# A new issue plan for a fused macaron block: the sums of squares placed behind GpSimd's additions, the copies of V's windows one step earlier

## The chip, the cores and the metric

One core of one Trainium2 chip. The metric is the device time of one execution in microseconds (us), the median of several runs. The engines are PE (TensorE; its weight loads are listed as PEld), DVE (VectorE), ACT (ScalarE), POOL (GpSimd) and SP (SyncE, which issues nearly all DMAs here). Each engine runs its own instructions strictly in the order in which the program lists them, and waits at an instruction until the semaphores that it names are reached.

## The reference: what is computed

`x` is 2048 tokens by 128 features. Three blocks are added to it in turn: half of a 6-layer local-attention transformer, a linear-attention block with a GELU feed-forward, and half of the same 6-layer transformer again (the same weights). So there are 12 attention layers, 6 before the linear block and 6 behind it.

```python
x = x + 0.5 * ffn_ref(layernorm(x), ...)    # 6 layers
x = x + attn_ref(layernorm(x), ...)         # linear attention, ELU+1 features
x = x + 0.5 * ffn_ref(layernorm(x), ...)    # 6 layers
# one layer of ffn_ref: 16 heads of 64, window 32
q, k, v = split(shift_tokens(x) @ Wqkv)
q, k = l2norm(q) * qs, l2norm(k) * ks ; rotary tables on both
out = local_attention(q, k, v)    # a window sees itself and the one before
x = out @ Wo + x
x = (a * gelu(gate)) @ W2 + b2 + x          # a, gate = LN(shift(x)) @ W1 + b1
```

Everything is fp32.

## The kernel before, in words

**Tiling.** Features lie on the partitions, tokens along the free dimension. A layer is worked off in 8 chunks of 256 tokens (`c`), a chunk in 4 steps; a step is one half of the heads (`h8`) of one tile of 128 tokens (`t`). So a layer has 32 steps. Feed-forward and norms go by chunks of 512 tokens (`f`).

**What one chunk does**, with the plan's names in brackets:

- `project` [proj], lines 274-324: Q and K by 8 matmuls per call, the rotary products on DVE (L298), their additions on POOL (L304), the squares on ACT (L310), the addition of the two halves of the squares on POOL (L324).
- `square_sums` [ss], L326-336: 4 matmuls add the squares over each head. `norms`, L398-412: the inverse root on ACT and DVE. `spread_norms` [rk], L428-442: two small DMAs to DRAM (L434), four back that spread them (L439).
- `gather` [gq0, gq1], L390: two DMAs of 256 KB each put the rotated queries into head order (`hq`). `scale_keys` [sk0, sk1]: one DVE multiplication (L448), then four DMAs of 128 KB (`hk`, L396).
- `values_proj` [vproj]: V by matmul (L348), copied by ACT (L352). `values_windows` [vwin], L354-375: eight DMAs (L368-L371) that copy V into the layout of the windows (`vw`, two buffers).
- `similarities` [sim], `exponentials` [e0, e1], `normalised` [nrm], `transposed` [te], `values` [av] and `output` [out]: scores on PE (L476, L486), maxima on DVE (L498), exponentials on ACT (L511), their scaling on POOL (L523), transposes on PE (L536), the product with V on PE (L563, which reads `vw`), the projection by `wo` (L579), and the residual on DVE (L588). In a layer's last call `output` also loads the next layer's `wo` (L136).
- `feed_forward` [ff, ff2, ff3] in 17 pieces; its norm has the mean (L211), the square on ACT (L215) and the variance matmul (L218).

**What sets the order.** No scheduler moves anything: the order is written out by hand in the table `POS`. A piece with the entry `(s, p)` goes to step `t0 + s`, and within a step the pieces are issued in the order of `p`:

```python
def at(step, pos, fn, *args):
    plan.setdefault(step, []).append((pos, len(plan.get(step, ())), fn, args))
...
put("ss", t0 + 2 * g2, square_sums, l, c, g2)
put("vwin", t0 + 2 * t, values_windows, l, c, t)
...
for step in sorted(plan):
    for _, _, fn, args in sorted(plan[step], key=lambda it: it[:2]):
        fn(*args)
```

`p` only ranks pieces; a changed `p` matters where it moves a piece past another one that uses the same engine (or issues a DMA on SP, or takes a PSUM buffer from the same pool of five, `ps_small`). SP's list holds 34 DMAs per chunk, and each DMA also waits for the one eight places ahead of it to land, because eight semaphores are used in turn. Between layers 5 and 6 lie the linear block's pieces `sums0`-`sums3`, `kv`, `outs0`-`outs3`; this stretch is called the hand-over below.

Of the kernel before, what the change touches and what calls it, by code (L numbers as in the profile page):

```python
# [30 lines left out]
HID = 512  # L31
LN_EPS = 1e-5
POS = {
    "tabq": [(-11, 115), (-10, 177)],
    "tabk": [(-9, 9), (-9, 156)],
    "ss": [(-7, 141)],
    "vwin": [(1, 68)],
    "gq0": [(-6, 126)],
    "gq1": [(-4, 58)],
    "e0": [(0, 84)],  # L40
    "e1": [(0, 85)],
    "nrm": [(1, 67)],
    "qn": [(-3, 111)],
    "ek": [(-1, 82)],
    "proj": [(-9, 137), (-8, 31), (-8, 32), (-8, 33), (-8, 37), (-8, 140)],
    "vproj": [(-2, 21), (-2, 80)],
    "norms": [(-4, 35), (-4, 73), (-4, 110)],
    "rk": [(-4, 193), (-3, 20)],
    "sk0": [(-2, 81)],
    "sk1": [(-1, 83)],  # L50
    "te": [(2, 53), (2, 55)],
    "av": [(2, 132), (2, 179), (2, 180)],
    "out": [(4, 71), (4, 119)],
    "sim": [(0, 65), (0, 66), (0, 67)],
    "ff": [(11, 88), (12, 26), (12, 92), (13, 5), (13, 159), (14, 93), (15, 128), (15, 148),
        (16, 13), (17, 108), (17, 125), (18, 23), (18, 47), (18, 48), (18, 151), (21, 131),
        (21, 187)],
    "ff2": [(12, 113), (13, 16), (13, 168), (14, 57), (14, 163), (15, 103), (15, 133), (16, 39),
        (16, 105), (16, 108), (16, 109), (16, 185), (16, 189), (17, 28), (17, 63), (17, 86),
        (17, 89)],  # L60
    "ff3": [(10, 171), (10, 172), (10, 174), (10, 182), (10, 186), (10, 190), (11, 2), (11, 14),
        (11, 19), (11, 27), (11, 112), (11, 114), (11, 117), (11, 124), (11, 142), (11, 170),
        (11, 170)],
    "start0": [(-19, 75), (-16, 60), (-16, 77), (-16, 90), (-13, 30), (-11, 130)],
    "start1": [(-10, 134), (-9, 145), (-7, 87), (-7, 146), (-7, 154), (-6, 12)],
    "start2": [(-8, 56), (-7, 62), (-5, 36), (-5, 192), (-4, 96), (-4, 165)],
    "start3": [(-4, 34), (-4, 38), (-4, 79), (-4, 107), (-3, 4), (-3, 22)],
    "sums0": [(-9, 18), (-9, 104), (-8, 122), (-8, 155), (-8, 161), (-7, 61), (-7, 123),
        (-6, 24)],
    "sums1": [(-1, 106), (-1, 178), (0, 64), (0, 69), (1, 6), (1, 66), (2, 150), (2, 172)],  # L70
    "sums2": [(1, 173), (1, 188), (2, 157), (2, 191), (3, 54), (3, 129), (3, 149), (4, 100)],
    "sums3": [(3, 183), (4, 11), (4, 43), (4, 70), (4, 72), (4, 120), (4, 120), (4, 181)],
    "kv": [(5, 3)],
    "outs0": [(5, 8), (5, 10), (5, 74), (5, 97), (5, 139), (5, 166), (6, 59), (6, 176), (7, 158),
        (7, 162), (8, 51), (8, 52), (8, 121), (8, 135)],
    "outs1": [(6, 50), (11, 46), (11, 99), (12, 15), (13, 1), (13, 44), (13, 169), (14, 42),
        (14, 152), (15, 25), (15, 41), (15, 98), (15, 138), (16, 40)],
    "outs2": [(6, 144), (13, 74), (13, 95), (13, 153), (14, 101), (14, 136), (14, 167), (15, 45),
        (15, 127), (15, 184), (16, 76), (16, 78), (16, 116), (17, 29)],
    "outs3": [(5, 118), (15, 164), (16, 17), (16, 102), (17, 49), (17, 91), (18, 7), (18, 94),  # L80
        (18, 151), (19, 47), (19, 143), (19, 147), (19, 160), (19, 175)],
}
EXP_LN = "natural_log_exp_and_others"

# [867 lines left out]
```

## Time and profile before

| | |
|---|---|
| median of 3 runs | 3533.92 us (3528.49 to 3537.05) |
| the profiled execution's own time | 3530.32 us |
| its span, first to last instruction | 3528.3 us |
| granted TensorE clock, mean | 0.979 |
| DVE, ACT, POOL busy | 74%, 78%, 63% of the span |
| one step, from one layer's `wo` load to the next (629.20 to 898.12 us, 32 steps) | 8.40 us |
| mean time of one DMA issue on SP | about 0.6 us (L368 to L371: medians 554 to 595 ns) |

The waits view names for each engine what it waited for, with the sum, the count and the longest. The timeline lists instructions in order of time: start, duration, engine, line, operation, output<-input, and in brackets the idle time before it and what ended that. On SP the duration is that of issuing a DMA, not of its landing.

### The profile page before, as it was taken

What the parts mean: (1) busy time and instruction counts of PE and PEld (TensorE: products, weight loads), DVE (VectorE), ACT (ScalarE), POOL (GpSimd) and SP (SyncE); (2) the same over time, 40 slices, a digit from 0 to 9 for tenths busy, and PEclk for the clock granted to TensorE, in tenths of its full rate; (3) what the DMA queues carried; (4) which work ended last, traced back from release to release, by engine and by line L of the source; (5) the groups of instructions that cost most, each with busy time, mean ns of one, the idle gap of its engine ahead of it and who ended that gap; (6) DMA issues with size and microseconds to landing.
All of it is one profiled execution on the core that took longest, in us unless ns stands there. A gap on an engine that the chain in (4) does not pass through costs nothing. (4 is left out here: it accounts for less than half of the span.)

```text
span 3528.3 us, 153591 instructions
## 1 busy us (share of the span) xinstructions
PE 3300.5 (94%) x64088; PEld 2299.6 (65%) x64088; DVE 2623.4 (74%) x4924; ACT 2738.8 (78%) x8805; POOL 2228.7 (63%) x2195
## 2 busy tenths in 40 slices
PE   6999999999999999998677999999999999999997
PEld 3766666666666676676335766766666766766664
DVE  5777877777777787786337777877778777777784
ACT  3787877888887887887546788888888788888886
POOL 5676666667666667663136666666667676666661
PEclk8999999999999999999789999999999999999999
DMA  4555565556556556555003556555565565565552
GB/s 121 132 147 139 128 149 144 130 144 150 130 145 148 132 143 151 137 130 129 24 12 94 138 138 147 134 142 143 134 154 133 135 156 135 134 154 131 137 137 72
DMA packets 356445, 459.91 MB, mean 130 GB/s; under 512 B 52396, under 2 KB 218664, under 8 KB 355752
## 3 DMA queue, kind: packets, MB, share of 16 engines
q1 hardware_dynamic: 355752, 450.11, 52.4%
q8 instruction: 504, 8.26, 1.0%
q14 instruction: 189, 1.55, 0.1%
HBM read 96.53 MB, written 2.62 MB: 28 GB/s over the span
## 5 line engine op out<-in xcount | busy, mean ns | idle before, releaser
L511 ACT ACTIVATE e<-sim,st,rq 128x64 f32<-128x64 f32 x3072 | 1194.8, 411 | 307.4 <-DVE st L499 294.5
L298 DVE TENSOR_TENSOR prod<-p,tab 128x1024 f32<-128x1024 f32 x768 | 933.3, 1220 | 196.9 <-ACT sq L310 100.8
L304 POOL TENSOR_TENSOR abq<-prod 128x512 f32<-128x512 f32 x384 | 491.4, 1280 | 743.9 <-DVE prod L298 625.0
L289 PE MATMUL p<-xa,wqk 128*128 128x256 f32 x3072 | 783.7, 399 | 12.0 <-DVE xa L243 6.4
L324 POOL TENSOR_TENSOR sq<-sq 128x256 f32<-128x256 f32 x768 | 669.9, 892 | 1.0
L511 ACT ACTIVATION_READ_ACCUMULATOR e<-sim,st,rq 128x1 f32 x3072 | 649.4, 211 | 0.0
L289 PEld LDWEIGHTS p<-xa,wqk 128*128 128x128 f32 x3072 | 563.7, 193 | 104.0 <-issue 11.2
L310 ACT ACTIVATE sq<-p 128x512 f32<-128x512 f32 x768 | 438.3, 611 | 217.0 <-PE ss L332 109.6
L304 POOL TENSOR_TENSOR abk<-prod 128x512 f32<-128x512 f32 x384 | 496.1, 1292 | 117.2 <-DVE prod L298 113.4
L563 PEld LDWEIGHTS av<-eT,vw 64*64 64x64 f32 x18432 | 397.3, 135 | 196.1 <-DVE xf L588 34.1
L523 POOL TENSOR_TENSOR e<-e,st 128x512 f32<-128x512 f32 x384 | 400.2, 1042 | 137.7 <-DVE st L521 113.1
L348 PE MATMUL pv<-wv,xa 128*128 128x512 f32 x768 | 415.0, 622 | 60.7 <-ACT gate L619 57.1
L563 PE MATMUL av<-eT,vw 64*64 64x32 f32 x18432 | 442.6, 221 | 30.7 <-DMA vw<-v 13.0
L579 PE MATMUL y<-oT,wo 128*128 128x128 f32 x3072 | 394.1, 282 | 0.2 <-DVE oT L572 0.2
L563 PE MATMUL av<-eT,v 64*64 64x32 f32 x6144 | 392.6, 220 | 1.0 <-issue 0.9
L579 PEld LDWEIGHTS y<-oT,wo 128*128 128x128 f32 x3072 | 357.7, 192 | 18.6 <-issue 1.0
L448 DVE TENSOR_TENSOR abk<-abk,rk 128x1024 f32<-128x1024 f32 x192 | 349.3, 1819 | 2.9 <-issue 0.7
L498 DVE TENSOR_REDUCE sim<-sim 128x4 f32<-128x256 f32 x768 | 309.4, 403 | 29.0 <-PE sim L486 28.7
L486 PE MATMUL sim<-hk,hq 64*32 64x64 f32 x24576 | 330.9, 223 | 0.0
L536 PEld LDWEIGHTS te<-sq_consts,e 128*128 128x128 f32 x1536 | 188.6, 141 | 210.9 <-issue 156.1
L563 PEld LDWEIGHTS av<-eT,v 64*64 64x64 f32 x6144 | 325.9, 135 | 0.0
L572 DVE COPY oT<-av 128x256 f32<-128x256 f32 x384 | 161.3, 420 | 211.9 <-PE av L563 207.1
(139 smaller groups left out, 4574.3 us busy)
## 6 DMA issues: line engine op xcount, KB each, us to landing
hq<-abq SPq DMA_DIRECT2D x384, 256.0 KB
hk<-abk SPq DMA_DIRECT2D x768, 128.0 KB
vw<-v SPq DMA_DIRECT2D x768, 128.0 KB
rk<-rkd SPq DMA_DIRECT2D x384, 128.0 KB
vw<-v SPq DMA_DIRECT2D x744, 64.0 KB
wqk<-in_Wqk SPq DMA_DIRECT2D x48, 256.0 KB
tab<-in_rot SPq DMA_DIRECT2D x24, 512.0 KB
wv<-in_Wv SPq DMA_DIRECT2D x24, 256.0 KB
```

Of the source, the lines that this page charges most:

```text
L289: nc.tensor.matmul(both[s][:, u, :], wqk[g][:, 2 * s + u, :], xs, start=True, stop=True)
L298: nc.vector.tensor_tensor(prod, both[s].unsqueeze(2).to_broadcast([P, 2, 2, AC]), tabs[l, s].rearrange("p (u v) t -> p u v t", u=2), ALU.mult,
L304: nc.gpsimd.tensor_tensor(d["qk"[s], g // 2][:, :, g % 2, :], prod[:, 0], prod[:, 1], ALU.add)
L310: nc.scalar.activation(sq, both[s], AF.Square)
L324: nc.gpsimd.tensor_tensor(sq[:, 0, :], sq[:, 0, :], sq[:, 1, :], ALU.add)
L348: nc.tensor.matmul(ps, xa[:, ti * P : (ti + 1) * P], wv[j], start=True, stop=True)
L448: nc.vector.tensor_tensor(k, k, r.unsqueeze(1).to_broadcast([P, 2, CH]), ALU.mult)
L486: nc.tensor.matmul(sims[par][WIN * b : WIN * b + WIN, i, :], d["hq"][rows, 4 * h8 + i, at : at + WIN], d["hk"][rows, 4 * h8 + i, at : at + ...
L511: nc.scalar.activation(e[:, i, par, :], d["sims", step][par][:, i, :], AF.Exp, bias=st8[:, 0, i, par : par + 1], scale=rq[:, i, par : par ...
L523: nc.gpsimd.tensor_tensor(ef, ef, st8[:, 1].rearrange("p i r -> p (i r)").unsqueeze(2).to_broadcast([P, 8, SK]), ALU.mult,)
L563: nc.tensor.matmul(av[u][r : r + 64, m, WIN * b : WIN * b + WIN], d["vs", t][u][b][:, at : at + DH], d["eT", step][64 * u : 64 * u + 64, i ...
L579: nc.tensor.matmul(y[:, 0:P], wo[:, i, :], d["oT", t].rearrange("p h u m q -> p (h u m) q")[:, i, :], start=(i == 0), stop=(i == 7),)
```

## The change

Only the table `POS` changes. Many ranks are merely renumbered. What lies at another place in the step, or in another step, is below (the pieces that every chunk uses, and the pieces of the feed-forward, the start and the linear block whose order against others changes):

```diff
-    "ss": [(-7, 141)],
-    "vwin": [(1, 68)],
-    "gq0": [(-6, 126)],
+    "ss": [(-7, 188)],
+    "vwin": [(0, 68)],
+    "gq0": [(-6, 87)],
...
-    "sk1": [(-1, 83)],
+    "sk1": [(-1, 164)],
...
-    "out": [(4, 71), (4, 119)],
+    "out": [(4, 100), (4, 120)],
...
-    "ff": [(11, 88), (12, 26), (12, 92), (13, 5), (13, 159), (14, 93), (15, 128), (15, 148),
+    "ff": [(11, 88), (12, 30), (12, 92), (13, 5), (13, 156), (14, 94), (15, 128), (15, 144),
...
-    "start2": [(-8, 56), (-7, 62), (-5, 36), (-5, 192), (-4, 96), (-4, 165)],
+    "start2": [(-9, 163), (-7, 35), (-5, 41), (-5, 192), (-4, 9), (-4, 111)],
...
-    "outs1": [(6, 50), (11, 46), (11, 99), (12, 15), (13, 1), (13, 44), (13, 169), (14, 42),
-        (14, 152), (15, 25), (15, 41), (15, 98), (15, 138), (16, 40)],
-    "outs2": [(6, 144), (13, 74), (13, 95), (13, 153), (14, 101), (14, 136), (14, 167), (15, 45),
-        (15, 127), (15, 184), (16, 76), (16, 78), (16, 116), (17, 29)],
+    "outs1": [(6, 51), (11, 85), (11, 99), (12, 15), (13, 1), (13, 47), (13, 167), (14, 46),
+        (14, 148), (15, 29), (15, 45), (15, 98), (15, 137), (17, 44)],
+    "outs2": [(6, 105), (13, 74), (13, 95), (13, 149), (14, 96), (14, 161), (14, 165), (14, 183),
+        (15, 103), (15, 127), (16, 75), (16, 77), (16, 117), (17, 33)],
```

Set side by side, the two programs hold the same instructions. In the order of each engine: on PE 49 of 37,494 rows stand elsewhere, 44 of them variance matmuls of the feed-forward's norm (L218) that now precede the eight `y` matmuls (L579) instead of following them; on DVE 15 of 4,926, on ACT 6 of 5,735, on POOL 27 of 2,200 (24 of them are the zero fills of `vw`, L366; all other moves on these three engines lie at the start and around the hand-over); on SP at least 1,188 of 3,405. The 4 matmuls of `ss` stand at the same place of PE's order as before, except three times in the hand-over. SP's order for one chunk, by steps modulo 4 (8+4 means so many DMAs):

| step | before | after |
|---|---|---|
| 0 | gq1 2, rk to DRAM 2 | gq1 2, **vwin of tile 0: 8**, rk to DRAM 2 |
| 1 | rk back 4, vwin of tile 0: 8 | rk back 4 |
| 2 | sk0 4, gq0 2 (a layer's `wo` load ahead of them) | **vwin of tile 1: 8**, sk0 4, gq0 2 (the `wo` load behind them) |
| 3 | vwin of tile 1: 8, sk1 4 | sk1 4 |

## The prediction

> **What bounds the kernel now.** I read the page first, then PE's busy time by stretches, then what PE waited for, then the timeline of SP, because the edits move mostly DMAs.
>
> The page's first part and two stretches from the view by windows (columns: time, PE, PEld, DVE, ACT, POOL busy with counts, clock, DMA share, GB/s):
>
> ```profile
> PE 3300.5 (94%) x64088; PEld 2299.6 (65%) x64088; DVE 2623.4 (74%) x4924; ACT 2738.8 (78%) x8805; POOL 2228.7 (63%) x2195
> ```
> ```profile
> 400.00:700.00 300.00, 290.15 (x5847) 206.44 (x5845) 232.76 (x442) 248.16 (x802) 199.67 (x196) 1.00 0.57 139
> ...
> 1640.00:1940.00 300.00, 229.56 (x2344) 129.28 (x2342) 154.13 (x260) 165.13 (x393) 117.09 (x120) 0.85 0.21 52
> ```
>
> PE is busy 290 of 300 us in the layers, but only 230 of 300 around the hand-over. So an edit in the layers is worth at most the gaps that it closes on PE, about 3% of the stretch. The waits view of PE says who ended those gaps (sum, times, longest):
>
> ```profile
> PE pv L348 <- ACT gate L619: 57.1, 75, 1.4
> PE ss L332 <- POOL sq L324: 30.5, 21, 5.3
> ...
> PE av L563 <- DMA vw<-v: 13.0, 16, 1.6
> ```
>
> The reader sees three candidates. The first is a PSUM buffer that the GELU frees; no edit touches it. The second is the wait that the change's name speaks of; in the layers it is small (3.4 us between 100 and 1640, 2.7 us between 1940 and 3440; the rest lies at the start, 17.0, and in the hand-over). The third is the copy of V's windows, and it is an edit's target. The timeline of SP shows why `vw` comes late:
>
> ```profile
> 600.34 1.17 SPq L390 DMA_DIRECT2D hq<-abq  x2
> 601.56 0.71 SPq L368 DMA_DIRECT2D vw<-v  x1
> ...
> 607.24 0.59 SPq L371 DMA_DIRECT2D vw<-v  x1
> 607.93 2.53 SPq L396 DMA_DIRECT2D hk<-abk  x4
> 610.56 1.90 SPq L390 DMA_DIRECT2D hq<-abq  x2
> 612.56 1.92 SPq L434 DMA_DIRECT2D rkd<-rn  x2
> 615.85 2.09 SPq L439 DMA_DIRECT2D rk<-rkd  x4
> ```
>
> `vw` of tile 1 stands behind gq0 (600.34), whose buffer comes free only when the scores of step 3 are done. Its last DMA is issued from 607.24 to 607.83, and `av`, which reads it, starts at 611.02: 3.2 us for a landing. The chain of waits has two such landings, of 2.37 and 4.26 us, so the lead is used up:
>
> ```profile
> 1938.28 2.37 DMA vw<-v
> 1940.65 0.04 issue
> 1940.69 1.01 PE av L563 x54
> ```
>
> **The change, part by part.**
>
> *ss.* Its four matmuls follow the same PE instruction as before in every layer; what it was moved past (copies of `av` on ACT and DVE, L570 and L572) are other engines' work. Cost 0; below nothing and above it too, because PE's order and POOL's additions are the same.
>
> *vwin one step earlier.* No instruction is added; eight DMAs per tile leave their place. Tile 1 now stands behind rk's return (ends 617.94) and ahead of sk0, so it needs only the copy of V and the `av` of step 1 that frees its buffer; it is ready about 1.5 steps, 12 us, sooner. Tile 0 stands behind gq1 instead of behind rk's return, some 6 us sooner by the rows above. Queued behind it on SP are the `rkd` DMAs, which need DVE's `rn`. Eight issues of 0.6 us are 4.8 us; with vwin of tile 1 gone from in front of sk1, sk1 and gq1 can go once DVE's multiplication is done (603.5), so gq1 ends about 607.3 and vwin at 612.1, against 612.56 for `rkd` today. So nothing behind it is later. What goes: PE's 13.0 us on `vw`. Ends: 0 (the next of `av`'s inputs, `eT` or a PSUM buffer, is as late) and 13.0. PE's own previous instruction had ended before each of these gaps and DVE's `eT` appears with only 4.3 us over 5 gaps, so I take **-11**. ACT also waited 33.2 us for `vw` (its copy of V must not overwrite a buffer that is still being read) and POOL 112.1; both engines are idle over 20% of the span, so these count 0 in the sum and are kept for a rival.
>
> *sk1, gq0.* DVE's order is unchanged. sk1's four DMAs stand eight issues nearer the front, gq0 waits for the same scores as before. 0.
>
> *The variance matmul ahead of `y`, 44 times.* Its input, ACT's `lnsq`, ends 2.6 us before the `y` that it now precedes. `y` ends 1.0 us later (the matmul's length), and behind it DVE's residual add. The timeline of DVE shows the cover:
>
> ```profile
> 644.54 0.59 DVE L588 TENSOR_TENSOR xf<-y,xa 64x128 f32<-64x128 f32 x2
> 646.87 0.42 DVE L572 COPY oT<-av 128x256 f32<-128x256 f32 x1 [1.74 <-PE av L563]
> ```
>
> DVE idles 1.74 us right after it; 0.7 us of cover remains. Cost 0; without that cover it would be 44 times 1.0 us on DVE, not on PE. PSUM buffers change owners with this swap: some `av` now take the one that ACT's copy of V frees, whose end is over 1 us ahead of `av` in the median step of those classes. 0.
>
> *The zero fills of `vw` on POOL*: 24 of 0.516 us, earlier by five POOL instructions, in a step without `ss`. 0.
>
> *The next layer's `wo` load*, moved from ahead of sk0 to behind gq0. Today it is issued at 629.20, the moment the last `y` of the layer ends; gq0's two DMAs follow until 635.61. The first `y` of the next layer starts at 642.45, now 643.5 because the variance matmul precedes it. That leaves 7.8 us for a landing that by the trace's semaphore updates takes 3.7 to 5.6 us today. Lower end: 0. Upper end: it queues fully behind gq0's transfers, 3.90 us for one landing in the chain, so 7.6 to 9.5 us and up to 1.7 us late, ten times, 17 us. I take 0, since landings overlap in every stretch of the SP timeline. The Trainium skill (DMA: Bandwidth & Descriptors, section Anatomy of one DMA — SWDGE path) fits a DMA as 2.0 us plus bytes at 436 GB/s; if that held here, gq0's 512 KB ahead and 512 KB of `wo` would make an estimate of 4.4 us and no wait at all. The trace's 3.7 to 5.6 us for `wo` alone is already above the page's 3.2, so the sum goes by the rows and their upper end stays in the range.
>
> *The start.* DVE's subtraction for chunk 2 (0.69 us) goes ahead of two rotary products and POOL's product for it ahead of two additions. From 26.16 to 35.21 POOL runs without a gap, so DVE's 0.69 us is hidden; later, POOL's additions of squares gain what the earlier one loses. 0, between -1 and +2.
>
> *The hand-over.* Three edits weigh. The variance of chunk 2 goes into the 3.26 us in which `ss` waits for POOL (1820.73 to 1824.62): -1.9. DVE's add of chunk 2's result is put ahead of two rotary products, so DVE stands from 1839.2 until that matmul is done (about 1846.4) and the products come some 8 us later; the second `ss` of chunk 6_0 follows about 3 us later, but `rn` no longer queues behind two `xa` writes (2.35 us) and catches up. The last chunk's variance goes ahead of a projection; its norm today holds DVE for 5.18 us before 1889.24, and with it the products that lead to the first scores. Adding these up along the timeline I get the first exponentials about 3 us sooner. Ends: -6 (all three gains) and +8 (the products' delay in full). I take **-3**.
>
> **Sum.** The profiled run took 3530.3; -11 - 3 gives 3516.3. The median shown is 3.6 us above that run, so on its footing 3520. About 0.3%, 10.6 us, is what a measurement of this kernel can tell from no change.
>
> **Rivals.**
>
> 1. *The gaps refill.* `av` waits instead for `eT` or the V copy, and the hand-over costs its upper end: -3 + 8 or so, no measurable change, 3530. For it: only 13 us were ever at stake, and PE waits for a PSUM buffer in 75 places. Against it: the waits on `eT` are a third as long in total.
>
> 2. *More is gained.* ACT's 33.2 us of waiting on `vw` delay exponentials and GELUs, and those free the buffers of the 57.1 us row; if 20 us of it goes too, 3500. The Trainium skill (Perfetto Trace Analysis, section Identifying the Most-Contended Engine) says that matmul busy time is no measure of PE's headroom and that weight-load time is. Here that is 65%, which would allow more than PE's visible gaps. The trace speaks against: in the layers almost every gap has another name than `vw`, and the 57.1 us recur at the GELU, one or two per chunk of 512 tokens, also where no V copy waited.
>
> 3. *The `wo` load is late* (slower). It decides from the point where `wo` lands over 7.8 us after its issue. At 10.3 us, 2.5 us late in ten layers, the loss is 25 us: 3545; from there on the kernel is measurably slower. For it: the load moved 6.4 us behind and lies behind 512 KB. Against it: no landing of it above 5.6 us.
>
> 4. *It does not do what it says.* `ss` does not move on PE at all, so whatever happens comes from the DMAs and the hand-over. That is part of the forecast.
>
> **How the numbers follow.** Forecast (3510 to 3530) 0.57, of which 0.41 below 3523.3 and 0.16 above; refill 0.18; more gained 0.12; `wo` late or a like stall 0.13. So faster 0.53, within 0.3% 0.34, slower 0.13. The range leaves out the deepest part of rival 2 and most of rival 3: 3500 to 3541.
>
> **What would show it.** Right: PE's row `av <- DMA vw` under 2 us; SP issuing `vw` straight behind gq1 and behind rk; ACT's wait on `vw` gone; the layer at 268 us instead of 268.9; PE busy in 1640:1940 some 3 us more. Wrong: a row `y <- DMA wo`, `rkd` issued later than `rn` by a new SP queue, or a new wait in front of `av` of the size of the old one.

## The result, and the profile after

| | before | after |
|---|---|---|
| median, same chip | 3531.20 us (4 runs, 3526.18 to 3537.05) | 3511.79 us (4 runs, 3510.59 to 3512.60) |
| profiled run / its span | 3530.32 / 3528.3 us | 3511.34 / 3509.5 us |
| lead of the last `vw` copy's issue (its end) over the first matmul of `av`, median of tile 0 / tile 1, smallest | 4.4 / 3.1, -1.2 us | 13.3 / 17.9, 7.4 us |

The ratio is 0.9944 (95% interval 0.9927 to 0.9962): 19 us or 0.56% faster, against a forecast of 3520 us in a range of 3500 to 3541.

First PE's busy time on the page of after:

```profile
PE 3300.0 (94%) x64088; PEld 2303.4 (66%) x64088; DVE 2631.7 (75%) x4924; ACT 2735.9 (78%) x8805; POOL 2227.4 (63%) x2195
```

It is as long as before (3300.5 us). The span is 18.8 us shorter, so in the balance all that went is time in which PE stood still. The view by windows of after, for the two stretches that the prediction shows of before:

```profile
400.00:700.00 300.00, 291.18 (x5872) 205.94 (x5872) 238.88 (x442) 247.11 (x808) 200.74 (x198) 0.99 0.57 138
1640.00:1940.00 300.00, 232.15 (x2406) 130.30 (x2404) 159.05 (x265) 167.78 (x414) 123.16 (x125) 0.86 0.23 56
```

PE is busy 1.0 and 2.6 us longer in them. For the second one that is little evidence of a shorter hand-over: after is some 12 us ahead when it ends, so it holds later work. The waits of PE in after (sum, times, longest):

```profile
PE pv L347 <- ACT gate L618: 54.2, 74, 1.4
PE ss L331 <- POOL sq L323: 29.6, 22, 3.9
...
PE av L562 <- DVE eT L541: 10.0, 11, 2.5
...
PE av L562 <- issue: 3.4, 6, 1.1
```

The row `av <- DMA vw` (13.0 us) is gone. `av` waits longer for `eT` (4.3 us before), but not at the places where it had waited for `vw`: 8.9 of the 10.0 us lie in one step, the 24th of a layer, where the next layer's first projections begin. Before had other names for its gaps there, among them waits without a named end:

```profile
PE av L563 <- issue: 8.8, 7, 3.0
```

In that step PE's waits for `eT`, for the copy of `oT` and without a named end add up to 14.3 us in before and to 16.1 in after. The row of the change's name moved by 0.9 us. SP's timeline of after shows the new place of the copies: straight behind rk's return, ahead of sk0, with the `wo` load behind gq0:

```profile
606.80 2.17 SPq L438 DMA_DIRECT2D rk<-rkd  x4
610.72 0.58 SPq L367 DMA_DIRECT2D vw<-v  x1
...
615.86 0.59 SPq L370 DMA_DIRECT2D vw<-v  x1
621.29 2.54 SPq L395 DMA_DIRECT2D hk<-abk  x4
625.48 1.17 SPq L389 DMA_DIRECT2D hq<-abq  x2
626.70 0.70 SPq L135 DMA_DIRECT2D wo<-in_Wo  x1
```

**Where in time it was gained.** The start of the same exponential in both traces tells how far after is ahead. It is 1.2 us ahead at 121 us, 6.8 at 193, 9.4 at 281 (all within layer 0); 7.9 at the end of layer 5; 8.2 at layer 6's first exponentials; 17.3 ninety microseconds later; 19.4 near the end (3430 us). So nearly everything was gained in two *ramps*, the first sixteen steps of layer 0 and of layer 6, and nothing in the layers between. (The last 2.6 us of layer 0 lie at its end, where before's PE waited 2.95 us once; a second profile of before waited 1.22 us there.) In the ramps the steps hold no feed-forward yet and are short: after needs 7.3 us for each of the 8 steps from 127 to 186 us, against 8.4 us in the other layers. SP's list per chunk is as long as ever, so `vw` runs out of lead there first. It is tile 0 that does: in before its median lead over tiles 1 to 7 of the two ramps is 0.4 us, against 4.7 in the other layers, while tile 1 keeps 3.0 against 3.1. Its copies stand behind rk's return, and here they are issued until the moment at which `av` waits:

```profile
1931.01 1.73 SPq L439 DMA_DIRECT2D rk<-rkd  x4
...
1938.28 0.59 SPq L371 DMA_DIRECT2D vw<-v  x1
```

Of PE's 13.0 us on `vw`, 10.0 belong to tile 0.

Before's ramps lost more than the gaps on `vw` (7.8 us in the two). Windows of before, around one such wait (`av` at 153.88 us waited 1.25 us):

```profile
150.00:155.00 5.00, 3.63 (x80) 3.32 (x80) 3.55 (x9) 3.18 (x16) 4.34 (x4) 0.95 0.55 129
155.00:160.00 5.00, 5.00 (x54) 3.65 (x50) 2.48 (x3) 2.30 (x8) 1.28 (x1) 0.71 0.41 86
```

The reader is to look at the clock, the third number from the end: behind the gap it falls to 0.71 over 5 us, although PE is busy throughout. Layer 6 shows the same. Before, and then after, which is 17 us ahead by then:

```profile
1970.00:1975.00 5.00, 3.39 (x74) 2.84 (x73) 2.88 (x6) 3.95 (x18) 3.28 (x3) 0.88 0.60 135
1975.00:1980.00 5.00, 5.00 (x87) 3.71 (x86) 2.94 (x3) 1.56 (x3) 1.68 (x2) 0.78 0.20 42
```
```profile
1952.00:1957.00 5.00, 5.00 (x117) 3.74 (x110) 3.90 (x9) 3.42 (x13) 3.67 (x4) 1.00 0.71 173
```

Summed over layers 0 and 6, PE's gaps fell from 15.2 to 9.6 us and from 17.7 to 10.6 us, 12.7 of the 19.0 us by which these layers are shorter. The rest looks like the clock: the time at half clock fell from 10.2 to 4.1 us and from 13.7 to 0.9 us, which is worth at most half of it, 9.5 us. But only three stretches of before, of 3.4 us each, stand behind gaps of PE (154.5, 273.9 and 1973.8 us); 10.2 of layer 6's 13.7 us are one stretch at its very beginning (1895.3 us). And in the kernel with the copies alone (the first experiment) layers 0 and 6 are 16.7 us shorter, of which gaps make 12.5 us and half clock at most 1.5 (20.9 us of it in the two, against 23.9 in before). So the shorter ramps don't rest on the clock. What else made PE's work shorter in them is not shown.

### The profile page after: what moved, and what is told of

Its sections match the earlier page's. It is cut to its first block, busy times and chain, and to the rows that moved or that the text cites. A ratio compares the mean times of both kernels' runs of the same rounds, so it can differ in the third digit from the quotient of the medians.

```text
span 3509.5 us, 153525 instructions
## 1 busy us (share of the span) xinstructions
PE 3300.0 (94%) x64088; PEld 2303.4 (66%) x64088; DVE 2631.7 (75%) x4924; ACT 2735.9 (78%) x8805; POOL 2227.4 (63%) x2195
## 5 line engine op out<-in xcount | busy, mean ns | idle before, releaser
L347 PE MATMUL pv<-wv,xa 128*128 128x512 f32 x768 | 419.5, 628 | 55.4 <-ACT gate L618 54.2
L485 PEld LDWEIGHTS sim<-hk,hq 64*32 64x32 f32 x24576 | 305.9, 105 | 0.9 <-issue 0.6
```

The costliest lines, as they stand in the source:

```text
L347: nc.tensor.matmul(ps, xa[:, ti * P : (ti + 1) * P], wv[j], start=True, stop=True)
L485: nc.tensor.matmul(sims[par][WIN * b : WIN * b + WIN, i, :], d["hq"][rows, 4 * h8 + i, at : at + WIN], d["hk"][rows, 4 * h8 + i, at : at + ...
```

## The experiments

Every ratio is to the kernel before on the same chip. The experiments ran on three chips, on which its medians were 3532.7 to 3537.9 us.

| kernel | median us | ratio (95%) | layer 0, layer 6 | mean of eight layers | layer 5 with hand-over |
|---|---|---|---|---|---|
| before | 3531.2 | 1 | 263.1, 263.7 | 269.75 | 477.0 |
| before once more | 3536.0 (one run) | - | 260.5, 264.3 | 269.87 | 480.2 |
| after | 3511.8 | 0.9944 (0.9927-0.9962) | 254.0, 253.8 | 269.82 | 476.2 |
| `vwin` alone | 3510.5 | 0.9925 (0.9911-0.9939) | 254.9, 255.2 | 268.98 | 474.7 |
| after without `vwin` | 3550.9 | 1.0033 (1.0021-1.0045) | 261.6, 262.2 | 271.94 | 482.1 |
| output edit alone | 3551.4 | 1.0033 (1.0023-1.0044) | 260.3, 261.8 | 271.47 | 480.4 |
| `wo` load alone | 3541.7 | 1.0023 (1.0010-1.0036) | 263.6, 260.1 | 270.87 | 481.5 |
| variance ahead of `y` alone | 3534.3 | 1.0001 (0.9987-1.0015) | 260.6, 260.2 | 270.54 | 480.6 |
| start and linear block alone | 3543.2 | 1.0012 (1.0001-1.0023) | 264.6, 263.0 | 270.04 | 482.8 |
| `ss` alone | 3524.4 | 0.9975 (0.9962-0.9989) | 262.3, 262.8 | 270.57 | 475.5 |

The last three columns are from the one profile of each kernel: from a layer's first exponential to the next layer's; the eight layers are 1 to 4 and 7 to 10. Single profiles of kernels that should not differ in a column do so by some 4.5, 0.8 and 7.5 us, so only the ramps are told apart by them alone. Step by step more can be told: in the mean of the eight layers no kernel's step differs from before's (mean of its two profiles) by over 0.3 us, except the fourth and the sixth, where the `wo` load is late and the copies too (see 7), and the 21st to the 25th, around the boundary to the next layer.

**1. The copies of V alone (v_only).**

```diff
-    "vwin": [(1, 68)],
+    "vwin": [(0, 68)],
```

> The kernel before with one entry changed: the copies of V's windows one step earlier. Only SP's order and the place of POOL's 24 zero fills change. Theory A (the gain lies in the two ramps, the first eight or so steps of layer 0 and of layer 6, where the steps are short and the copies' lead before av is used up; in the layers between, nothing is gained because other waits take the small gaps): PE's row av <- DMA vw gone, the lead over before grows by some 5 us between 120 and 195 us, by some 8 us between 1900 and 1980 us, and stays level elsewhere; in all -12 to -16 us. Rival B (the start and hand-over edits make most of it, by getting the first exponentials out sooner): -2 to -6 us here. Rival C (the prediction's step: 11 us over the whole span, a share of it in the layers): -11 us, with 4 to 5 us of it outside the ramps.

Measured: 27 us faster, well above the 16 us that theory A allowed. PE's and ACT's rows on `vw` are gone. All four kernels with the earlier copies (two more follow) have layers 0 and 6 of 253.0 to 255.2 us, all ten without them 260.1 to 264.6 us: some 8 us per ramp, 16 together, as theory A says. The other 10 us, which theory A did not expect, are not located. In the one profile the eight layers are 0.8 us shorter each, most of it in the 23rd and 24th step, but that is no more than single profiles differ by, and the kernel of 9, about as fast, has layers of 269.70 us. Rivals B and C fall.

**2. After with the copies put back (v_undone).**

```diff
-    "vwin": [(0, 68)],
+    "vwin": [(1, 68)],
```

> The changed kernel with the copies of V's windows put back one step later; all other edits stay. Theory A: PE's waits on vw come back at the ramps with some 2.8 us at the start and 5 us behind the hand-over, and the kernel is only 3 to 7 us faster than before. Rival B: it keeps most of the gain, 13 us or more faster than before.

Measured: 13 us *slower* than before. PE's row on `vw` is back at 15.4 us over 17 times. So the other edits cost, which no theory said, and within the change the copies are worth 0.33 + 0.56 = 0.89%, some 31 us. The next two kernels were run with these to find the cost.

**3. The output edit alone (o_only).**

```diff
-    "gq0": [(-6, 126)],
+    "gq0": [(-6, 87)],
-    "out": [(4, 71), (4, 119)],
+    "out": [(4, 99.5), (4, 119)],
```

> The kernel before with the first output call of each pair moved behind the feed-forward piece and behind gq0: the variance matmul ahead of y 44 times, and the wo load behind gq0's two DMAs. The prediction costs both at 0. Theory A: within 2 us of before, DVE's wait of xf on y at some 40 us over 45 places, no row y <- DMA wo. Rival (the later wo load or the later y costs time that the copies of V pay back): 5 us or more slower, with a wait of y on wo. Rival (the swap itself closes the gap of some 3 us at the V copy near 270 us): 2 to 5 us faster.

Measured: 13.5 us slower. `y` waited for `wo` only once, for 0.2 us, so the later load is not late for its own reader. ACT's row `v <- DMA vw` grew from 33.2 to 54.0 us.

**4. The start and the linear block alone (h_only).** After with `vwin`, `ss`, `sk1`, `gq0` and `out` put back, each at the rank that restores before's order:

```diff
-    "ss": [(-7, 188)],
-    "vwin": [(0, 68)],
-    "gq0": [(-6, 87)],
+    "ss": [(-7, 139.5)],
+    "vwin": [(1, 68)],
+    "gq0": [(-6, 126)],
...
-    "sk1": [(-1, 164)],
+    "sk1": [(-1, 82.5)],
...
-    "out": [(4, 100), (4, 120)],
+    "out": [(4, 71.5), (4, 120)],
```

> The changed kernel with the copies of V, ss, sk1, gq0 and the output call put back: what is left of the change are the edits of the start and of the linear block. Prediction: 0 at the start and -3 us in the hand-over. Theory A: the first exponentials of layer 6 come 0 to 1.5 us sooner, the start gains some 1 us, in all 0 to -3 us. Rival B: -8 us or more, with the lead built up before the first av of layer 6.

Measured: some 4 us slower, at the edge of what can be told from nothing. PE's row on the squares is the longest of all kernels:

```profile
PE ss L331 <- POOL sq L323: 37.4, 20, 5.0
```

Between 1820 and 1965 us it holds 15.0 us, against 7.8 in before.

**5. What DVE and POOL do to each other between layers (before_again, t_only).** Kernel 3 also had PE gaps of 2.4 to 2.5 us, `p <- DVE oT`, 12.7 us over 6 times. They stand behind a meeting at the layer's boundary. The timeline of before, DVE and POOL:

```profile
530.87 1.27 POOL L304 TENSOR_TENSOR abq<-prod 128x512 f32<-128x512 f32 x1
531.84 1.38 DVE L448 TENSOR_TENSOR abk<-abk,rk 128x1024 f32<-128x1024 f32 x1
532.09 2.25 POOL L304 TENSOR_TENSOR abk<-prod 128x512 f32<-128x512 f32 x1
```

and the same place in the kernel with the output edit:

```profile
530.92 1.27 POOL L304 TENSOR_TENSOR abq<-prod 128x512 f32<-128x512 f32 x1
531.89 4.97 DVE L448 TENSOR_TENSOR abk<-abk,rk 128x1024 f32<-128x1024 f32 x1
532.14 1.27 POOL L304 TENSOR_TENSOR abk<-prod 128x512 f32<-128x512 f32 x1
533.37 1.05 POOL L523 TENSOR_TENSOR e<-e,st 128x512 f32<-128x512 f32 x1
...
534.37 1.41 POOL L324 TENSOR_TENSOR sq<-sq 128x256 f32<-128x256 f32 x2
...
537.25 0.48 PE L289 MATMUL p<-xa,wqk 128*128 128x256 f32 x1 [2.50 <-DVE oT L572]
```

DVE starts 0.97 us behind POOL's `abq` in both. In the first POOL waits a microsecond; in the second DVE's multiplication stands until POOL's last addition has ended (535.8), and PE then waits 2.5 us for the copy queued behind it. Theory D was that this draw, not the output edit, makes the loss. It was tried by a second profile of before, and by moving POOL's scaling of the query table so that `abq` ends sooner:

```diff
-    "tabq": [(-11, 115), (-10, 177)],
+    "tabq": [(-11, 115), (-10, 75)],
```

> The kernel before once more, for a second profile on the chip on which the others of this call run. Between layers, DVE's scaling of the keys (abk<-abk,rk) meets POOL's string of additions (abq, abk, e, sq): in the profile of before POOL's abk waits 8 times of 10 (2.25 us instead of 1.27) and DVE's scaling twice (4.97 and 3.5 us instead of 1.38), and PE then waits 2.4 us for a PSUM buffer (p <- DVE oT) and runs 3.4 us at half clock. Theory D (which of the two waits falls out anew in each execution, and each loss of DVE costs about 4 us): a profile some 8 us longer than 3530 us shows two to three more such losses. Rival E (DVE's losses are the output edit's doing): again two or fewer.

> The kernel before with one other entry changed, which the change doesn't touch: POOL's scaling of a layer's query table (four instructions, 1.83 us) goes ahead of the feed-forward's xc instead of behind it, into POOL's idle 1.79 us. POOL's abq addition then ends before DVE's scaling of the keys begins. Theory D: no scaling over 3 us at the ten boundaries, no row p <- DVE oT of 2.4 us, and 4 us per loss that before has on this chip, so 5 to 15 us faster than before. Rival E: within 3 us of before, because in before DVE hardly loses.

Measured: before once more lost 5 of 10 draws, and its span was 5.5 us longer than in the first profile, which had lost 2. So the draw does fall out anew. In these two profiles it cost less than theory D's 4 us per loss: two of the three new losses lie in the eight layers of the table, which are 0.12 us longer each, 1 us in all. But the table's edit gave 0.9998 (0.9986 to 1.0011): four losses remained. The table's load landed too late for the earlier place (at 2622 us POOL waited 2.56 us for it), so the edit didn't take the meeting away.

**6. The table's edit on both kernels (v_t, o_t).** The line above, added to kernels 1 and 3.

> Both: the copies of V's windows one step earlier and the query table's scaling ahead of xc. Theory A with D: the ramps' 14 to 16 us and the boundaries' losses add up, so 25 to 35 us faster than before (ratio 0.990 to 0.993), and no longer than the copies of V alone. Rival: the boundary only moves its loss elsewhere, no faster than the copies of V alone (26 us).

> The output call and gq0 moved as in the change, with the query table's scaling ahead of xc. It tells whether the 12 us that the output edit alone lost are its own. Theory D (they are losses of DVE at the boundaries, six in the profile): within 3 us of the kernel with the table's edit alone. Rival E (the swap of the variance matmul and y, or the later wo load, costs 12 us by itself): 8 us or more slower than that kernel.

Measured: 0.9917 (0.9902 to 0.9933), not to be told from the copies alone, and 1.0031 (1.0020 to 1.0042), as slow as the output edit alone, 9 us slower than the table's edit. So theory D falls as the explanation of that loss. In the first kernel the table's load is early enough, but its scaling now meets another multiplication of DVE and takes 3.33 us instead of 1.83, and DVE still lost five of ten draws behind it:

```profile
1323.08 1.78 DVE L448 TENSOR_TENSOR abk<-abk,rk 128x1024 f32<-128x1024 f32 x1
1323.77 3.33 POOL L263 TENSOR_SCALAR tab<-tab,qks 128x256 f32<-128x256 f32 x4
```

**7. The two halves of the output edit (o_wo, o_var).** Comparing the kernels of 2, 3 and 6 that hold the output edit with before step by step gave the next theory: each had one step 1.1 to 1.5 us longer, the fourth of every layer but 0 and 6, just behind the `wo` load. To move the load alone, it goes behind the generator's stop, and gq0 ahead of that:

```diff
-    "gq0": [(-6, 126)],
+    "gq0": [(-6, 87)],
...
-        if t == 1 and c == NAC - 1 and l + 1 < 2 * DEPTH:
-            wo = load_o(l + 1)
         yield
+        if t == 1 and c == NAC - 1 and l + 1 < 2 * DEPTH:
+            wo = load_o(l + 1)
```

> The kernel before with the wo load alone moved behind gq0 (ten DMAs on SP in all; the variance matmul stays behind y). Theory F (the load then stands straight ahead of the eight copies of V on SP, the copies end later, ACT's next copy of V waits for them, and behind it in ACT's order the exponentials wait): ACT's row v <- DMA vw grows from 33 to some 54 us, the step behind the load is 1.0 to 1.5 us longer in each layer, in all 6 to 9 us slower. Theory G (the cost of the output edit is that of the variance matmul ahead of y): no change, ACT's row stays at 33 us.

The other half, on before:

```diff
-    "out": [(4, 71), (4, 119)],
+    "out": [(4, 99.5), (4, 119)],
```

> The kernel before with the variance matmul alone moved ahead of y (44 times; the wo load stays ahead of gq0, behind sk0). The prediction costs it at 0, because DVE idles 1.74 us behind the residual. Theory F: DVE's wait of xf on y at some 37 us, and 0 to 5 us slower, all of it at the layers' boundaries (the steps 22 to 24), where DVE has no such idle time. Theory G: 10 to 14 us slower.

Measured: the load alone is 9 us slower, the variance alone 1.0001. Theory F holds. ACT's row in before and in the kernel with the load alone, and PE's row in the latter:

```profile
ACT v L352 <- DMA vw<-v: 33.2, 31, 4.0
```
```profile
ACT v L352 <- DMA vw<-v: 61.6, 44, 4.2
```
```profile
PE y L579 <- DMA wo<-in_Wo: 3.0, 5, 0.8
```

and ACT's timeline behind the load of layer 3 (issued at 637.88 us, the copies of V straight behind it) shows the wait that holds the exponentials:

```profile
645.26 0.59 ACT L352 COPY v<-pv 128x512 f32<-128x512 f32 x1 [1.93 <-DMA vw<-v]
```

In layers 1 to 4 and 7 the fourth step takes 8.3 to 9.1 us there, 7.4 to 7.8 in before and 7.4 to 7.5 with the copies alone. In the mean of the eight layers it is 1.3 us longer than in before, and the sixth step gives 0.5 us of that back. PE's own gaps in the fourth and fifth step grew by 5.4 us over ten layers; where the rest of the 9 us lies is not shown. In after the fourth step is 0.06 us longer than before in the mean of eight layers: with the copies earlier on SP nothing that matters stands behind the load. PE's row shows the prediction's third rival at work too: without the variance matmul in front, `y` comes 1.0 us sooner and the load, which lands 5.0 to 7.5 us after its issue in the layers, is late five times.

**8. The edit that names the change (ss_only).**

```diff
-    "ss": [(-7, 141)],
+    "ss": [(-7, 188)],
```

> The kernel before with only the edit that the change is named for: the sums of squares at rank 188 instead of 141. On PE three matmuls change places with ss, all in the hand-over; no other engine's order changes. Every theory: within 2 us of before, and the row ss <- POOL sq as long as before, near 30 us. If the named edit were what matters: 8 us or more faster.

Measured: 0.9975 (0.9962 to 0.9989), some 8 us faster: the reading that I held unlikely. PE's row on the squares is the shortest of all:

```profile
PE ss L332 <- POOL sq L324: 23.9, 19, 3.2
```

In the hand-over three `ss` change places with a matmul that used to follow them; at two of them the wait for POOL falls from 3.3 to 0.9 and from 1.7 to 0.8 us: 3.4 us. The rest of the 8 us is not shown: the profiled run (3535.7 us) was the slowest of its twelve, whose median is 3524.4, so its trace can't show where the others gained.

**9. The copies of V, and the meeting at the boundary taken away (v_t2).** Table loaded and scaled two steps earlier, in 11 layers:

```diff
-    "vwin": [(1, 68)],
+    "vwin": [(0, 68)],
+    "tabq1": [(-13, 115), (-12, 177)],
...
-        put("tabq", base, tables, l, 0)
+        put("tabq1" if l else "tabq", base, tables, l, 0)
```

> The copies of V one step earlier, and in 11 of the 12 layers the query table loaded two steps earlier and scaled on POOL two steps earlier, in a stretch of 3.4 us in which POOL idles and DVE has no scaling of keys. Theory D in its mended form (DVE and POOL bar each other where their instructions on SBUF meet; ahead of xc the table's scaling met the other scaling of the keys and took 3.33 us instead of 1.83, so nothing was won): no scaling of keys over 3 us at a boundary, p <- DVE oT under 3 us in all, and 3 to 10 us faster than the copies of V alone (ratio 0.990 to 0.9915). Rival (PE fills the boundary with other waits anyway): ratio 0.992 to 0.993 as with the copies of V alone.

Measured: no lost draw and no wait `p <- DVE oT`, as asked for, and 0.9931 (0.9913 to 0.9949), no better than the copies alone. PE waits for `eT` instead, against 8.8 us with the copies alone:

```profile
PE av L564 <- DVE eT L543: 17.0, 14, 2.5
```

The three kernels with the copies and without the output edit (0.9917 to 0.9931) lie below after (0.9944), but the intervals overlap. That one of them beats after is not shown; the single entry `vwin` reaches about as much as the whole change.

## Why the prediction held, step by step

The sign and the range held. The sum of -14 us came out as -19: by the experiments on single edits, the large term `vwin` was too small, `ss` brought a gain where nothing was expected, and other edits that were priced at nothing cost some of it again.

- **`vwin`, -11: right mechanism, mis-sized.** It is worth 27 us alone and some 31 within the change. The step that failed is the upper end: 13.0 us, PE's row alone, with "both engines are idle over 20% of the span, so these count 0 in the sum". In layers 0 and 6 PE's gaps shrank by 12.7 us where its row on `vw` has 7.8, and ACT waited 18.0 of its 33.2 us on `vw` there, with the exponentials queued behind that wait; its idle share over the whole span says nothing on that. How much of the ramps' gain is ACT's and how much PE's own is not separated. In the eight layers between, where ACT waited 14.6 us, the 0 was right: after's layers without that wait are no shorter. This is the second rival's mechanism, but not its reason: the row `pv <- ACT gate` that it counted on hardly moved (57.1 to 54.2 us).
- **Its place.** The timeline that explains the late copies is tile 1's, but 10.0 of the 13.0 us were tile 0's. The forecast of its move was right: tile 0 was to be some 6 us sooner and tile 1 some 12, and their leads grew by 8.9 and 14.8 us. The layer was to shrink to 268 us. From one `wo` load to the next (626.70 to 895.35) after has 268.65 against 268.92 us, and the mean of eight layers did not shrink. The gain was in the ramps, where four of before's waits on `vw` lie in each (7.8 of the 13.0 us). The prediction had these sixteen waits and didn't ask when they occur.
- **The `wo` load, 0: right for the change, for a reason the prediction did not give.** Alone it costs 9 us, mostly not by its landing but by pushing the copies behind it. The prediction priced the load's own reader and not the queue behind the load. With `vwin` moved ahead of it, the fourth step is as short as before. In after's layers the load lands 4.4 to 7.2 us after its issue, slower than the 3.7 to 5.6 us that the prediction took over from before, but within its 7.8 us of room.
- **The variance ahead of `y`, 0: right.** Alone 1.0001. DVE's new wait on `y` (35.9 us over 49 times, 37.5 in after) is covered as the prediction's timeline shows.
- **sk1 and the zero fills, 0:** not run by themselves. The fills go with `vwin` in every kernel, and besides after only the kernel of 2 has sk1's move.
- **`ss`, 0, and the hand-over, -3.** PE's order with `ss` does change in the hand-over, and that is worth 0.25%. The prediction had one of these swaps, -1.9 us, under the hand-over, and it measured -2.4. The other edits of start and linear block cost about 4 us. Together that is -4, near the -3 forecast, but out of two terms the prediction did not have. In the two profiles after reaches layer 6's first exponentials only 0.3 us further ahead than it left layer 5.
- **The start, 0.** After is 1.2 us ahead by 91 us; two profiles of before differ by 1.9 us at that point, so this is not told from nothing.
- **Its marks.** Row `vw` gone, SP's places, ACT's wait gone, PE busy 2.6 us more in 1640:1940 (3 forecast): as said, though the last also follows from after being ahead when that window ends. No `y <- DMA wo` in after. The row on `eT` grew by 5.7 us, as the first rival has it, but in another step than the waits on `vw`, so this is no refill of those gaps.

The ratios of the single edits (`vwin`, output, start and linear block, `ss`) add up to -0.55%, the change has -0.56%. The agreement is partly luck: the cost of the output edit depends on `vwin`, as 7 shows, and each ratio is uncertain by some 0.1%. What stays open: where the 10 us of `vwin` alone outside the ramps lie, how the other 4 us of the ramps' 17 in that kernel came about, whether the layers of `vwin` alone are shorter than before's at all, and the rest of the gain of `ss`.

## What to carry to other kernels

Price a late transfer by every engine whose in-order queue stands behind it, not only by the bottleneck's own row; what is queued behind an early waiter counts, not that engine's idle share, and it counts where the steps have no slack (here in the ramps, not in the layers between). List *when* the waits of a row occur: of the 16 entries over 192 tiles, half lay in the two ramps, where the step is shorter and a fixed list of DMAs loses its lead. And run the edits of a mixed change one by one: here one entry brought 0.75%, another took back 0.33%, and the entry that the title names first brought 0.25%, of which two swaps in the hand-over show 3.4 us.

## What the runs showed of the hardware

- **The clock falls after short gaps, by a grid.** In after, each of the three gaps of 2.4 us at a boundary (527.9, 1067.3 and 2336.8 us) is followed within 1.5 us by a stretch of half clock; in before, the gap of 1.25 us at 153.88 us is (windows above). Not every such gap is: with the copies alone, one of two of 2.4 us, and before's gap of 3.15 us at 2091.0 us is not. The traces show what decides. In each of the fourteen, every stretch of half clock starts on one grid of 3.413 us that runs through the whole execution. With PE's idle time counted per cell of this grid, no cell at full clock with under 1.1 us of idle time is followed by half clock, and every one with over 2.0 us is (351 such starts in all). The gap of 1.25 us fell into one cell with 1.36 us of idle time in all; the gap of 3.15 us was split into cells with 1.95 and 1.20 us. The Trainium skill (TensorE: Matmul & The Clock Gate, section What's actually happening) gives a free-running window of 3413 ns and has the clock halve after an idle window. The window agrees with the traces; that PE must be idle for a whole one does not, since cells with as little as 1.15 us of idle time were followed by half clock.
- **DVE's and POOL's additions bar each other, and the loser can wait for a whole string.** DVE's 1.4 us multiplication took 4.97 us behind three more kinds of POOL instructions, four in all. Who loses is not set by the program: with the same offset of 0.97 us POOL lost in one profile and DVE in another, and in two profiles of the kernel before DVE lost two and five of ten draws. The Trainium skill (SBUF — State Buffer, section Who interferes with whom) tells of an exclusive lock, for which a DVE instruction with two SBUF inputs contends with a GpSimd instruction that reads SBUF, and says that issue order decides who blocks. That they exclude each other agrees with the trace. Here DVE's instruction started ahead of POOL's next one and still stood behind four of them.
